# Second biases of a routed layer as one bf16 product a node tile, the second list ahead of the own rows, chosen rows scaled on ScalarE

## The chip, the cores and the metric

The kernel runs on one core of one Trainium2 chip. The core has a matrix engine (TensorE, PE in the profile; its weight loads are PEld), a vector engine (VectorE, DVE), an activation engine (ScalarE, ACT), GpSimd (POOL), which also issues the indirect DMAs (gathers and scatters by a list of rows), and SyncE (SP), which issues the plain DMAs. TensorE writes its results to PSUM, which has eight banks of 128 x 512 float32 here; VectorE and ScalarE read them from there. The metric is the device time of one execution in microseconds (us), as the median over runs.

## The reference

There are 1250 nodes with 512 features and 41250 edges. First comes a graph network of two layers, each of which takes for every node the maximum over its neighbours and multiplies it and the node itself by weights. Then comes a layer with 8 experts, and this is what the change touches:

```python
logits = x_flat @ Wr
probs = jax.nn.softmax(logits, axis=0)
vals, idx = jax.lax.top_k(probs.T, C)            # C = 512 nodes for each expert
selected = x_flat[idx]
h = gelu(einsum('ecd,edf->ecf', selected, W1) + b1[:, None, :])
out_e = einsum('ecf,efd->ecd', h, W2) + b2[:, None, :]
weighted = vals[..., None] * out_e
output = zeros_like(x_flat).at[idx.reshape(-1)].add(weighted.reshape(-1, Dd))
```

`x_flat` is the layer-normed result of the graph network. So each expert chooses the 512 nodes with its highest probabilities, works on these rows alone (512 to 256, Gelu, 256 to 512), and adds its rows, scaled with the probability, to the nodes that they came from. The result is added to the node's own `x`. The second bias `b2` of an expert enters a node as probability times `b2`, for every expert that chose the node.

## The kernel before

**Stages.** `fast_gnn` computes the graph network and ends at about 674 us. It leaves the rows `xs` (the tile `acc` in the profile), their layer norm in memory (`y_d`), and its transpose `yT`. `expert_choice` (line 1479) does the rest. The 1250 nodes are cut into ten tiles of 125 rows (`NT`, `TN`). A second form of the program for unusual graphs (`general_gnn`) stands behind a branch and doesn't run here.

**Routing, 674 to 721 us.** The threshold of each expert is found in eight rounds (line 1553). Each round counts on VectorE, sums with a small TensorE product (`pn`) and goes on with a few small VectorE operations. Then `chosen` (a 0 or 1 for each node and expert), each chosen node's place, and the lists are made. Between these steps `beside()` puts a piece of other TensorE work: the dense expert.

**The dense expert.** Expert 0 is computed for all nodes (`DENSE = 1`), by the generator `dense_steps` (line 1416). Each of its last ten pieces makes one tile of 125 rows: a product that puts the bias into a PSUM bank (`self.bias`), two products in float32 that add to it, and a ScalarE copy into `head.res` (the tile `xh`). A float32 product of 512 columns shows as two entries of TensorE.

**The bias product.** `fb` holds the eight second biases three times (partitions 0, 32 and 64), `bp` is their split into three bf16 parts whose sum is the float32 value, and `pick` is a matrix of zeros and ones. `pick[:, e]` times `bp` writes the bias of expert `e` into all rows of a bank (line 1518).

**Own rows.** `own_row(t)` (line 1690) adds `gate` (probability where chosen) times the dense expert's rows to `xs` on VectorE and stores the tile to `out` by two SP DMAs, one of 112 and one of 13 rows.

**The chosen experts, 1 to 7.** `listed(e)` (line 1662) makes the list of an expert: `pays` and `oh` on VectorE, ten small TensorE products into `pi`, then `got`, `idx` (the nodes) and `val` (their probabilities) on VectorE. The probabilities go through as three bf16 parts, which lie in `pay4` next to the node's number. `gathered` (line 1682) issues four gathers of 128 rows each on POOL. `expert` (line 1702) is a generator of two halves. The first half transposes the rows (`pt`, two banks, copied by ScalarE to `yselT`) and makes the hidden values (`ph`, then Gelu to `hT`). The second half makes four tiles of 128 rows: the bias product and two float32 products into `po`, a VectorE product by `val` into `oo`, and a scatter on POOL that adds the rows to `out`. Scatters of an expert wait for those of the expert before, and the first ones for the stores of the own rows.

**What sets the order.** Every engine is wrapped by `InOrder` (line 24), which keeps its instructions in the order in which they are written. The loop at line 1748 writes, for each expert: first half, (for expert 1 alone) the rest of the dense steps and the ten own rows, the next expert's list and gathers, second half. The banks `po` and `ph` and the small results of routing all come from the pool `ps_m`, tile name `pm`, with four banks in turn (line 1501); a product into a bank waits until the last reader of the bank's former content is done. `ps_t` has two banks for the transposes.

In the profile nearly all instructions have line 34, that of the `InOrder` wrapper, so groups are told apart by tile names. Memory that is reused shows under an older name: `ohs`, `xh`, `wroot` and `acc` hold the routing's and the dense expert's data.

Of the kernel before, what the change touches and what calls it, by code (L numbers as in the profile page):

```python
# [9 lines left out]
F32 = mybir.dt.float32  # L10
# [1282 lines left out]
class Routing:  # L1293
# [122 lines left out]
    def dense_steps(self):  # L1416


        dve, act, pe, pool, sp = self.engines
        TN, rows, KC, FC = self.sh["TN"], self.sh["rows"], self.KC, self.FC  # L1420
        NT = len(rows)
        cuts = [0, 4, 7, NT]
        for e in range(DENSE):
            w1, w2 = self.dense[e]
            for n, (t0, t1) in enumerate(zip(cuts, cuts[1:])):
                c0, w = t0 * TN, sum(rows[t0:t1])
                early = e == 0 and n < 2
                while early and any(t not in self.have for t in range(t0, t1)):
                    yield
                if early:  # L1430
                    both = self.wide[n]()
                for f in range(FC):
                    ph = both[f] if early else self.bank()
                    for k in range(KC):
                        pe.matmul(ph[:, :w], w1[:, k, f * P:(f + 1) * P], self.yT[:, k, c0:c0 + w],
                                  start=(k == 0), stop=(k == KC - 1))
                        if k == 1:
                            yield
                    if early:
                        self.waiting.append((e, f, c0, w, ph))  # L1440
                    else:
                        self.hidden(e, f, c0, w, ph)
                    yield
            for t in range(NT):
                r = rows[t]
                po = self.bank()
                self.bias(po[:r], e, r)
                for f in range(FC):
                    pe.matmul(po[:r], self.hT[:, f, t * TN:t * TN + r], w2[:, f, :],
                              start=False, stop=(f == FC - 1))  # L1450
                act.copy(self.res[e][:r, t, :], po[:r])
                yield

# [20 lines left out]
    def beside(self, n=1):  # L1474
        for _ in range(n):
            next(self.steps, None)


def expert_choice(tc, ctx, sh, xs, yT, y_d, out, head, flags=None):
# [22 lines left out]
    ps_x = ctx.enter_context(tc.tile_pool(name="ps_x", bufs=1, space=PSUM))  # L1502


    B3 = 96
    fb = rp.tile([P, D], F32, name="fb")
    pool.memset(fb[:B3], 0.0)
    for g in range(3):
        sp.dma_start(fb[32 * g:32 * g + E, :], sh["fb2"])
    bp = rp.tile([P, D], BF16, name="bp")  # L1510
    pick = rp.tile([P, E, P], BF16, name="pick")
    pool.memset(pick[:B3], 0.0)
    for g in range(3):
        pool.affine_select(out=pick[:B3], in_=pick[:B3], compare_op=ALU.not_equal, fill=1.0, base=-32 * g,
                           pattern=[[-1, E], [0, P]], channel_multiplier=1)

    def bias(po, e, r):
        pe.matmul(po, pick[:B3, e, :r], bp[:B3, :], start=True, stop=False)

    head.bias = bias  # L1520
    head.bank = lambda: ps_m.tile([P, D], F32, name="pm")

    weights = {}
# [158 lines left out]
    def gathered(idx):  # L1682
        ysel = rp2.tile([P, CC, D], F32, name="ysel")
        for c in range(CC):
            pool.indirect_dma_start(
                out=ysel[:, c, :], out_offset=None, in_=y_d[:, :],
                in_offset=bass.IndirectOffsetOnAxis(ap=idx[:, c:c + 1], axis=0))
        return ysel

    def own_row(t):  # L1690
        r = rows[t]
        for e in range(DENSE):
            dve.scalar_tensor_tensor(xs[:r, t, :], head.res[e][:r, t, :], gate[:r, t, e:e + 1], xs[:r, t, :],
                                     op0=ALU.mult, op1=ALU.add)
        cut = r - r % 16
        for p0, p1 in ((0, cut), (cut, r)):
            if p1 > p0:
                sp.dma_start(out[t * TN + p0:t * TN + p1, :], xs[p0:p1, t, :])
# [3 lines left out]
    def expert(e, idx, val, ysel):  # L1702
# [16 lines left out]
        yield  # L1719
        for c in range(CC):  # L1720
            po = ps_m.tile([P, D], F32, name="pm")
            bias(po, e, P)
            for f in range(FC):
                pe.matmul(po, hT[:, f, c * P:(c + 1) * P], w2[:, f, :],
                          start=False, stop=(f == FC - 1))
            oo = rp2.tile([P, D], F32, name="oo", bufs=4)
            dve.tensor_scalar_mul(oo, po, val[:, c:c + 1])
            add = pool.indirect_dma_start(
                out=out[:, :], out_offset=bass.IndirectOffsetOnAxis(ap=idx[:, c:c + 1], axis=0),
                in_=oo[:, :], in_offset=None, compute_op=ALU.add)  # L1730
# [13 lines left out]

    gate = rp.tile([P, NT, E], F32, name="gate")
    dve.tensor_mul(gate, chosen, pcol)
    beside(4)
    for e in range(DENSE, E):
        work = expert(e, *made, ysel)
        next(work)  # L1750
        if e == DENSE:

            for _ in head.steps:
                pass
            for t in range(NT):
                own_row(t)
        if e + 1 < E:

            made = listed(e + 1)
            ysel = gathered(made[0])  # L1760
        elif flags is not None:
            value = nc.values_load(flags[0:1, 0:1], min_val=0, max_val=1)
        next(work)
    return value

# [115 lines left out]
```

## Time and profile before

| what | value |
|---|---|
| median of 8 runs | 872.78 us (871.18 to 876.19) |
| the profiled execution's own time | 875.14 us |
| its span, first to last instruction | 873.4 us |
| mean granted clock of TensorE | 0.938 of full speed |
| busy: TensorE, VectorE, ScalarE, POOL | 697.3, 623.3, 208.6, 528.3 us |
| `oo` by VectorE, 28 of 128x512 | 21.0 us, 750 ns each |
| `hT` by ScalarE from PSUM, 14 of 128x512 | 9.6 us, 687 ns each |
| copies `xh<-pm` by ScalarE, 10 of 125x512 | 5.9 us, 586 ns each |
| scatters `out<-oo` on POOL, 28 | 44.8 us, 1601 ns each; the first expert's land in 5.4 to 6.0 us |
| last scatter issued | 858.02 us |

The profile is one execution of the program with all its instructions. Busy time counts an engine's running instructions; idle time in brackets, where a row has it, is the wait ahead of the instruction with what ended it. `out<-in` names the tile that is written and those that are read. The granted clock tells at which share of its full speed TensorE was let run.

### The profile page before, as it was taken

What the parts mean: (1) busy time and instruction counts of PE and PEld (TensorE: products, weight loads), DVE (VectorE), ACT (ScalarE), POOL (GpSimd) and SP (SyncE); (2) the same over time, 40 slices, a digit from 0 to 9 for tenths busy, and PEclk for the clock granted to TensorE, in tenths of its full rate; (3) what the DMA queues carried; (4) which work ended last, traced back from release to release, by engine and by line L of the source; (5) the groups of instructions that cost most, each with busy time, mean ns of one, the idle gap of its engine ahead of it and who ended that gap; (6) DMA issues with size and microseconds to landing.
All of it is one profiled execution on the core that took longest, in us unless ns stands there. A gap on an engine that the chain in (4) does not pass through costs nothing. (4 is left out here: it accounts for less than half of the span.)

```text
span 873.4 us, 8381 instructions
## 1 busy us (share of the span) xinstructions
PE 697.3 (80%) x2534; PEld 375.9 (43%) x2534; DVE 623.3 (71%) x1134; ACT 208.6 (24%) x349; POOL 528.3 (60%) x549
## 2 busy tenths in 40 slices
PE   0698867778888787998887889678668888999992
PEld 0344534444454433555444445334335544444440
DVE  6998799999999956469989899996543554332211
ACT  2644322334420132311100001002123322112110
POOL 7543777777777775077777777778701402566542
PEclk9999879999999798999999999989779899999997
DMA  7686557977877688258967878777731405777653
GB/s 173 201 263 205 131 176 173 229 227 239 260 221 225 190 257 264 70 182 179 226 212 221 275 242 282 239 224 256 241 114 48 146 0 170 185 174 186 125 98 51
DMA packets 67785, 165.47 MB, mean 189 GB/s; under 512 B 12918, under 2 KB 17588, under 8 KB 67730
## 3 DMA queue, kind: packets, MB, share of 16 engines
q0 software_dynamic: 37472, 114.19, 48.8%
q1 hardware_dynamic: 29438, 49.55, 17.5%
q10 hardware_dynamic: 820, 1.10, 0.5%
q8 instruction: 22, 0.36, 0.2%
q14 instruction: 33, 0.27, 0.1%
HBM read 136.35 MB, written 28.40 MB: 189 GB/s over the span
## 5 line engine op out<-in xcount | busy, mean ns | idle before, releaser
L34 POOL DMA_INDIRECT hb<-table_d,late_i x214 | 228.6, 1068 | 97.4 <-issue 56.3
L34 PEld LDWEIGHTS <-ohs 126*125 126x125 bf16 (+1 forms) x1221 | 169.0, 140 | 210.6 <-issue 134.0
L34 PE MATMUL pq<-xh,ohs 126*125 126x512 bf16 x816 | 202.7, 391 | 46.5 <-DVE acc L34 45.4
L34 POOL DMA_INDIRECT hb<-table_d,nat_i x140 | 147.4, 1053 | 60.2 <-issue 35.4
L34 DVE TENSOR_TENSOR acc<-acc,pq 125x1024 f32<-125x1024 f32 x122 | 148.6, 1218 | 25.1 <-PE pq L34 14.1
L34 PE MATMUL pair<-xh,ohs 126*125 126x512 bf16 x384 | 98.7, 395 | 28.2 <-DVE acc L34 28.2
L34 DVE TENSOR_TENSOR acc<-acc,pair 125x1024 f32<-125x1024 f32 x58 | 70.6, 1217 | 3.1 <-PE pair L34 0.4
L34 DVE TENSOR_TENSOR wide<-wide,hb 125x1024 f32<-125x1024 f32 (+1 forms) x60 | 71.4, 1189 | 1.8
L34 POOL DMA_INDIRECT ysel<-y_d,idx x28 | 27.7, 988 | 72.8 <-issue 29.7
L34 DVE TENSOR_TENSOR hb<-hb 125x1024 f32<-125x1024 f32 (+2 forms) x55 | 52.9, 962 | 22.1 <-DMA hb<-table_d,nat_i 14.6
L34 PE MATMUL pm<-wroot,turn 128*125 128x512 f32 x128 | 66.0, 600 | 0.4 <-ACT turn L34 0.4
L34 PE MATMUL pair<-wrel,turn 128*125 128x512 f32 x80 | 44.8, 712 | 13.0 <-ACT turn L34 9.8
L34 DVE TENSOR_TENSOR wide<-hb 125x1024 f32<-125x1024 f32 (+1 forms) x40 | 47.9, 1198 | 9.5 <-DMA hb<-table_d,nat_i 8.3
L34 POOL DMA_INDIRECT out<-oo,idx x28 | 44.8, 1601 | 15.8 <-DVE oo L34 8.1
L34 PE MATMUL pm<-yselT,w 128*128 128x512 f32 x112 | 49.9, 599 | 4.7 <-ACT yselT L34 4.7
L34 PE MATMUL pm<-w,hT 128*128 128x512 f32 x112 | 52.7, 591 | 0.0
L34 DVE TENSOR_SCALAR oo<-pm,val 128x512 f32<-128x512 f32 x28 | 21.0, 750 | 44.0 <-PE pm L34 44.0
L34 PE MATMUL pm<-wrel,turn 128*125 128x512 f32 x80 | 44.3, 706 | 4.5 <-DVE acc L34 4.5
L34 ACT COPY line<-pm 125x512 f32<-125x512 f32 x16 | 9.4, 585 | 114.9 <-PE pm L34 114.9
L34 DVE COPY got<-pi 128x20 f32<-128x20 f32 x7 | 1.2, 178 | 49.7 <-PE pi L34 49.7
L34 PEld LDWEIGHTS pm<-yselT,w 128*128 128x128 f32 x112 | 20.7, 190 | 29.8 <-issue 23.4
L34 PE MATMUL pair<-ident,acc 125*128 125x125 f32 x48 | 8.7, 312 | 31.1 <-DVE acc L34 15.5
(272 smaller groups left out, 919.5 us busy)
## 6 DMA issues: line engine op xcount, KB each, us to landing
w<-in_fw SPq DMA_DIRECT2D x14, 512.0 KB
ohs<-idx_d SPq DMA_DIRECT2D x10, 615.2 KB
root_d<-line SPq DMA_DIRECT2D x20, 250.0 KB
ahead<-root_d SPq DMA_DIRECT2D x20, 250.0 KB
table_d<-acc SPq DMA_DIRECT2D x20, 224.0 KB
ovf_d<-line SPq DMA_DIRECT2D x18, 224.0 KB
hb<-table_d,late_i POOLq DMA_INDIRECT x214, 4.8
ohs<-in_x SPq DMA_DIRECT2D x10, 250.0 KB
```

What stands on the lines that cost most here:

```text
L34: made = call(*args, **kwargs)
```

## The change

Three things change in `expert_choice` and `dense_steps`.

The bias products leave the dense steps and the chosen experts; there the first float32 product now starts the bank (`start=(f == 0)`), and `pick` goes. In their place each node tile gets one product: `shares` holds for every node the probabilities of the experts that chose it, as three bf16 parts, repeated three times in blocks of 32 columns. `shares` is transposed by ten products with a bf16 unit matrix `eye` into `sharesT`, by way of `ps_t` and ScalarE copies. `own_row(t)` multiplies `sharesT` of its tile with `bp`, which now holds each part of the biases three times, and adds the result (a bank of `ps_m`) to the rows. So a node gets the biases of all its experts at once, with its own row.

In the loop the list and the gathers of the next expert are written ahead of the rest of the dense steps and the own rows; for expert 1 this puts expert 2's list in front of them.

The chosen rows are scaled by ScalarE (`activation` with `Identity` and `scale`) in place of VectorE.

```diff
@@ dense_steps
                 po = self.bank()
-                self.bias(po[:r], e, r)
                 for f in range(FC):
                     pe.matmul(po[:r], self.hT[:, f, t * TN:t * TN + r], w2[:, f, :],
-                              start=False, stop=(f == FC - 1))
+                              start=(f == 0), stop=(f == FC - 1))
@@ expert_choice
+    assert 3 * E <= 32
     B3 = 96
     fb = rp.tile([P, D], F32, name="fb")
     pool.memset(fb[:B3], 0.0)
     for g in range(3):
-        sp.dma_start(fb[32 * g:32 * g + E, :], sh["fb2"])
+        for k in range(3):
+            sp.dma_start(fb[32 * g + E * k:32 * g + E * k + E, :], sh["fb2"])
     bp = rp.tile([P, D], BF16, name="bp")
-    pick = rp.tile([P, E, P], BF16, name="pick")
-    pool.memset(pick[:B3], 0.0)
-    for g in range(3):
-        pool.affine_select(out=pick[:B3], in_=pick[:B3], compare_op=ALU.not_equal, fill=1.0, base=-32 * g,
-                           pattern=[[-1, E], [0, P]], channel_multiplier=1)
-
-    def bias(po, e, r):
-        pe.matmul(po, pick[:B3, e, :r], bp[:B3, :], start=True, stop=False)
-
-    head.bias = bias
+    eye = rp.tile([P, P], BF16, name="eye")
+    pool.memset(eye, 0.0)
+    pool.affine_select(out=eye, in_=eye, compare_op=ALU.not_equal, fill=1.0, base=0,
+                       pattern=[[-1, P]], channel_multiplier=1)
+    shares = rp.tile([P, NT, 3, 32], BF16, name="shares")
+    pool.memset(shares, 0.0)
@@ own_row
         r = rows[t]
+        po = ps_m.tile([P, D], F32, name="pm")
+        pe.matmul(po[:r], sharesT[:B3, t, :r], bp[:B3, :], start=True, stop=True)
         for e in range(DENSE):
             dve.scalar_tensor_tensor(xs[:r, t, :], head.res[e][:r, t, :], gate[:r, t, e:e + 1], xs[:r, t, :],
                                      op0=ALU.mult, op1=ALU.add)
+        dve.tensor_add(xs[:r, t, :], xs[:r, t, :], po[:r])
@@ expert
             po = ps_m.tile([P, D], F32, name="pm")
-            bias(po, e, P)
             for f in range(FC):
                 pe.matmul(po, hT[:, f, c * P:(c + 1) * P], w2[:, f, :],
-                          start=False, stop=(f == FC - 1))
+                          start=(f == 0), stop=(f == FC - 1))
             oo = rp2.tile([P, D], F32, name="oo", bufs=4)
-            dve.tensor_scalar_mul(oo, po, val[:, c:c + 1])
+            act.activation(oo, po, AF.Identity, scale=val[:, c:c + 1])
@@ expert_choice, the end
     gate = rp.tile([P, NT, E], F32, name="gate")
     dve.tensor_mul(gate, chosen, pcol)
+    for i in range(3):
+        dve.tensor_tensor(shares[:, :, :, E * i:E * i + E],
+                          chosen.unsqueeze(2).to_broadcast([P, NT, 3, E]),
+                          pay4[:, :, :, 2 + i].unsqueeze(2).to_broadcast([P, NT, 3, E]), op=ALU.mult)
     beside(4)
+    sharesT = rp.tile([P, NT, P], BF16, name="sharesT")
+    for t0 in range(0, NT, KC):
+        n = min(KC, NT - t0)
+        pt = ps_t.tile([P, KC, P], F32, name="pt")
+        for k in range(n):
+            pe.matmul(pt[:B3, k, :], shares[:, t0 + k].rearrange("p j i -> p (j i)"), eye, start=True, stop=True)
+        act.copy(sharesT[:B3, t0:t0 + n, :], pt[:B3, :n, :])
     for e in range(DENSE, E):
         work = expert(e, *made, ysel)
         next(work)
+        if e + 1 < E:
+
+            made = listed(e + 1)
+            ysel = gathered(made[0])
+        elif flags is not None:
+            value = nc.values_load(flags[0:1, 0:1], min_val=0, max_val=1)
         if e == DENSE:
 
             for _ in head.steps:
                 pass
             for t in range(NT):
                 own_row(t)
-        if e + 1 < E:
-
-            made = listed(e + 1)
-            ysel = gathered(made[0])
-        elif flags is not None:
-            value = nc.values_load(flags[0:1, 0:1], min_val=0, max_val=1)
         next(work)
```

## The prediction

> **What bounds the kernel now.** I read the clock and the 40 slices first. In the last quarter TensorE is near full while VectorE falls to 1 to 3 tenths.
>
> ```profile
> PE   0698867778888787998887889678668888999992
> DVE  6998799999999956469989899996543554332211
> PEclk9999879999999798999999999989779899999997
> ```
>
> Next I read the timeline of a chosen expert in steady state. Columns: start, us, engine, operation.
>
> ```profile
> 764.51 0.38 PE L34 MATMUL pm<-bp,pick 96*128 96x512 bf16 x1
> ...
> 764.73 1.88 PE L34 MATMUL pm<-w,hT 128*128 128x512 f32 x4
> ...
> 766.45 1.04 PE L34 MATMUL pt<-ident,ysel 128*128 128x128 f32 x8
> 766.65 0.75 DVE L34 TENSOR_SCALAR oo<-pm,val 128x512 f32<-128x512 f32 x1 [1.18 <-PE pm L34]
> ...
> 767.14 1.07 ACT L34 COPY yselT<-pt 128x512 f32<-128x512 f32 x2 [7.80 <-PE pt L34]
> ...
> 767.78 1.14 PE L34 MATMUL pt<-ident,ysel 128*128 128x128 f32 x8 [0.29 <-ACT yselT L34]
> ...
> 769.60 7.13 PE L34 MATMUL pm<-yselT,w 128*128 128x512 f32 x16 [0.68 <-ACT yselT L34]
> ...
> 784.57 1.04 PE L34 MATMUL pt<-ident,ysel 128*128 128x128 f32 x8
> ```
>
> From 766.45 to 784.57 is one period, 18.12 us, and TensorE idles in it only about 1 us, for ScalarE's copies of the transposes (0.29 + 0.68). A bias product costs 764.73 - 764.51 = 0.22 us; four a period. The `oo` scaling on VectorE hangs beside this path.
>
> Then the place where the own rows and the second list lie:
>
> ```profile
> 721.27 0.23 DVE L34 TENSOR_TENSOR gate<-chosen,pcol 128x80 f32<-128x80 bf16 x1
> 721.62 4.73 DVE L34 SCALAR_TENSOR_TENSOR acc<-xh,gate,acc 125x512 f32<-125x512 f32 x7
> ...
> 728.79 0.75 DVE L34 SCALAR_TENSOR_TENSOR acc<-xh,gate,acc 125x512 f32<-125x512 f32 x1 [1.13 <-ACT xh L34]
> 729.46 0.36 DVE L34 TENSOR_TENSOR pays<-ohs,col 128x200 bf16<-128x200 bf16 x1
> 729.74 1.48 DVE L34 TENSOR_TENSOR oh<-ohs,lane 128x1280 bf16<-128x1280 bf16 x1
> ...
> 733.41 7.13 PE L34 MATMUL pm<-yselT,w 128*128 128x512 f32 x16 [0.67 <-ACT yselT L34]
> ...
> 740.39 0.40 PE L34 MATMUL pi<-pays,oh 128*128 128x20 bf16 x10
> ...
> 740.82 0.18 DVE L34 COPY got<-pi 128x20 f32<-128x20 f32 x1 [9.60 <-PE pi L34]
> 740.86 1.88 PE L34 MATMUL pm<-w,hT 128*128 128x512 f32 x4
> ```
>
> VectorE does all ten own rows while TensorE still works on the dense expert, then `pays` and `oh`, and then stands 9.60 us until TensorE reaches the list's product (`pi`), which is written behind expert 1's first half. So `got`, the list's next step, can't run before 740.8.
>
> Last, the granted clock by windows (columns: window, length, then busy time of each engine, clock):
>
> ```profile
> 688.00:693.00 5.00, 3.29 (x13) 1.89 (x13) 4.04 (x13) 0.68 (x6) 0.00 (x0) 1.00 0.02 7
> 693.00:696.40 3.40, 2.98 (x9) 2.11 (x10) 2.45 (x11) 0.83 (x5) 0.19 (x1) 0.51 0.00 0
> 696.40:699.80 3.40, 3.40 (x7) 1.96 (x8) 2.27 (x8) 0.41 (x1) 1.88 (x6) 0.50 0.00 0
> ...
> 716.80:720.20 3.40, 1.43 (x4) 0.35 (x2) 3.21 (x6) 0.59 (x1) 0.00 (x0) 1.00 0.01 2
> 720.30:723.70 3.40, 3.40 (x15) 1.75 (x16) 2.82 (x9) 0.00 (x0) 1.57 (x2) 0.51 0.13 36
> 723.80:727.20 3.40, 3.40 (x10) 1.53 (x9) 3.40 (x6) 1.18 (x2) 2.75 (x3) 1.00 0.87 275
> ```
>
> A stretch in which TensorE was busy for 1.43 of 3.40 us was followed by 3.4 us at half clock, one of 3.29 of 5.00 us by 6.8 us at half clock.
>
> **The change, part by part.** Times are those of the profiled execution, 875.14 us own time for a span of 873.4, 0.3% over the median of eight runs, 872.78; differences are carried over to the median.
>
> *Set-up.* Out go the memset of `pick` (0.95) and three selects (3.42) on POOL; in come an `eye` of 128 columns (an eighth of such a select and memset, about 0.3) and a memset of `shares`, 960 wide (0.9 by the 1024 of `pick`). SP issues 9 small loads instead of 3, 1.24/3 = 0.41 each, so 2.5 us more, and POOL's split of the bias (679.12 to 684.67) waits for them: it ends near 687 in place of 684.9. Behind it is only `pcol`'s memset, needed at 691.3; the expert weights behind the loads are needed at 733. Cost 0; if `pcol` were late, the excess over 4 us.
>
> *Dense bias products.* Ten of 0.22 leave TensorE. They count where a small product of the routing chain waited behind them: at 704.18 (its operand was ready at 703.17), 711.44, 713.54 and 715.82, so 4 x 0.22 = -0.9 us at the first list. The next three lie partly at half clock: -0.9 more on TensorE before expert 1's transposes.
>
> *`shares` and `sharesT`.* Three VectorE products of 240 bf16 elements, 0.4 each (0.36 for the 200 of `pays`, 0.48 for 320), after `idx`, in time VectorE now has free. Ten small TensorE products (under 0.1 each) and three ScalarE copies (0.59, 0.59, about 0.38) stand ahead of expert 1's transposes and use their two banks. Today the transposes wait for the gathered rows up to 732.11, the last landing 5.8 us after its issue beside the row stores; without these stores I take the median 3.9, so 725.3 + 3.9 = 729.2. Then the banks decide: dense work ends 726.5, three copies to 728.7, four transposes with copies behind them at about 0.9 to 731.9. The first half starts at 731.95 in place of 733.41: -1.5, and -0.9 if the landing stays late.
>
> *The list ahead of the own rows, and the rows' new product.* This is the dear part. The list moves `pays`, `oh`, ten TensorE products, `got`, `idx`, two `val` and four gathers ahead of ten rows. The gathers pass nothing on POOL and start 1.5 us earlier. On VectorE the rows now stand behind `got`, so behind TensorE's 740.39 - 1.5 = 738.9; `val` ends at 741.48 - 1.5 = 740.0. Each row is a multiply-add (0.68 to the next, 4.73/7) and a new add from PSUM (0.69 for 125x512 adds, 0.72 to a dependent one): 1.40, ten rows 14.0 us. Each row's bias product takes a `pm` bank, of which there are four, and the bank comes free only with the row's add. TensorE therefore advances one product per 1.40 us, and the first `po` of expert 1's second half needs the bank of row 7, free at 740.05 + 7 x 1.40 = 749.85. What is queued behind: the second half, and all later experts. It starts at 749.95 and takes 4 x 1.71 (1.93 less 0.22) = 6.8, ending 756.8, where expert 2's transposes began at 748.38. So +8.4 us at full clock, between +7.8 (rows at 1.36, by two independent pitches) and +9.7 (rows at 1.50, as `oo` takes 0.75 each, and only -0.9 before). The row stores on SP (20 x 0.41) end near 755 and land a few us later, so expert 1's scatters start near 758 in place of 746.5, take 4 x 1.9 and land 5.5 later, near 771; expert 2's scatters come at 776. SP's next weight load slips from 740.6 to about 755 for expert 4, which runs near 798. Both cost 0.
>
> *The clock after the stall.* For some 9 us TensorE does 0.22 in each 1.40, emptier than the stretch that halved the clock. When the second half starts the clock is half, and stays so 3.4 to 6.8 us by the two cases above; half of that is lost: +1.7 to +3.4, I take the middle, +2.6. It could be 0 if the clock held.
>
> The Trainium skill (TensorE: Matmul & The Clock Gate, part 1) has the clock halve after at least one idle window of about 3.4 us and return after one busy window. Read strictly, a stall with a product every 1.4 us is no idle window, and the sum without the clock term would be +4.5; the rows above show it halving with TensorE busy 1.43 of 3.40 us, so I go by the rows.
>
> *Experts 2 to 7.* 24 bias products less: 24 x 0.215 = -5.2. Of this the last expert's first is lost and some 0.1 elsewhere, since the second hidden half (849.25 + 0.69) is then what TensorE waits for: +0.3. `oo` on ScalarE: with `scale` from PSUM it lies between the copy's 0.59 and the identity's 0.81, nearest the Gelu's 0.69. The fourth one of an expert stands ahead of the next expert's first copy (766.65 + 0.62, its spacing, against 767.14): +0.15 on each of six transitions, 0.07 to 0.25 by the ends: +0.9. No table load stands before the identities after Sqrt or Exp; whether one is needed after Gelu no row shows. If so, two of 1.28 an expert fall into ScalarE's idle 3.85 and 7.8: 0 to +0.3. Sum -3.9 (-4.4 to -3.2).
>
> Together 8.4 + 2.6 - 3.9 = +7.1: own time 882.2, median 879.9.
>
> **The rivals.** *No stall* (ends faster): the rows' adds keep out of TensorE's way, by VectorE doing them in its idle time before 740. Then -1.5 - 0.9 - 3.9 = -6.3: 866.5. It decides if the rows are worked before `got`, or three banks more were there. For it: operands are ready by 729. Against: every engine follows the written order above. 10%.
> *Stall, but the clock holds or returns at once*: +4.5, 877.3. Against: 0.51 at 720 to 723.7. 18%.
> *Dearer*: rows at 1.50, a late first half, 6.8 us of half clock, poor gain after: 9.7 + 3.4 - 3.2 = +9.9, 882.7, more if weights or scatters slip past their margins of 5 us and more. 8%.
> *Bank wait partly covered*, so that stall and gain cancel (a stall near 5 us): within 0.2%, 4%.
>
> **How the numbers follow.** The forecast case (878 to 882) has 60%. The sound range is 874 to 884: below it lie "no stall" and half of the cancelling case, above it a part of the dearer one. 0.2% (1.75 us) is about what a measurement tells from no change: faster 0.11, same 0.04, slower 0.85.
>
> **What would show it.** Right: `got` of the second list ahead of the own rows, near 739; `pm<-bp` products spaced 1.4 us with TensorE idle for VectorE's add; half clock from about 750; a period of 17.4 in place of 18.12; no wait of the second scatters. Wrong: rows between 722 and 737, a table load in each expert, or a period that is not shorter because ScalarE's copies come later.

## The result and the profile after

The changed kernel takes 896.92 us (median of 16 runs, 891.36 to 902.35); the kernel before, run beside it, takes 872.37 (46 runs). The ratio is 1.0273 (95% interval 1.0257 to 1.029): 24 us slower. The direction was forecast, the size was not: the forecast was 879.9, with 884.0 as the upper end.

The profiled execution has a span of 895.6 us in place of 873.4, at a granted clock of 0.929 in place of 0.938. The 40 slices of the page of after (PE and DVE in tenths busy, the granted clock in tenths):

```profile
PE   0697976778898779997886896796688887878991
DVE  7898799999999856599997999976435625111100
PEclk9999889999999989999998999897888997988996
```

In the last nine slices TensorE has 7s and 8s where it had 8s and 9s, and the clock falls to 8 and 7 where it was 9. So the time was lost among the chosen experts. Four marks in both timelines cut the loss up:

| stretch | before | after | difference |
|---|---|---|---|
| first list's product to second list's product | 20.15 | 19.12 | -1.0 |
| second list's product to expert 2's transposes | 7.99 | 20.58 | +12.6 |
| expert 2's transposes to the last scatter's issue | 109.64 | 123.34 | +13.7 |
| first list's product to the last scatter's issue | 137.8 | 163.0 | +25.2 |

In this execution the graph stage also ended 3.7 us earlier (670.54 against 674.27), which has nothing to do with the change, and the routing took 0.7 us less; after the last scatter 16.8 us follow instead of 15.4. -3.7 - 0.7 + 25.2 + 1.4 = +22.2, the difference of the spans.

**The second stretch is the forecast stall.** The timeline of after around the own rows (start, us, engine, operation, and in brackets the idle time before it and what ended it):

```profile
734.92 0.40 PE L34 MATMUL pi<-pays,oh 128*128 128x20 bf16 x10
735.36 0.18 DVE L34 COPY got<-pi 128x20 f32<-128x20 f32 x1 [15.53 <-PE pi L34]
...
736.84 0.69 DVE L34 TENSOR_TENSOR acc<-acc,pm 125x512 f32<-125x512 f32 x1
737.44 0.75 DVE L34 SCALAR_TENSOR_TENSOR acc<-xh,gate,acc 125x512 f32<-125x512 f32 x1
...
737.58 0.38 PE L34 MATMUL pm<-bp,sharesT 96*125 96x512 bf16 x1 [1.34 <-DVE acc L34]
...
744.85 0.59 PE L34 MATMUL pm<-bp,sharesT 96*125 96x512 bf16 x1 [0.87 <-DVE acc L34]
...
746.31 9.36 PE L34 MATMUL pm<-w,hT 128*128 128x512 f32 x16 [0.87 <-DVE acc L34]
...
755.50 1.04 PE L34 MATMUL pt<-ident,ysel 128*128 128x128 f32 x8
```

The rows begin behind `got`, and TensorE gets one product per row: from 737.58 to 744.85 are five rows, 1.455 us each, and each product waits for VectorE's add (`<-DVE acc`). The second half starts 11.39 us behind the list's product and takes 9.36 us where the same sixteen entries elsewhere take 7.11. The windows over the stall (window, length, busy time of PE, PEld, DVE, ACT, POOL, then the granted clock, DMA share, GB/s) say why:

```profile
740.00:742.00 2.00, 0.59 (x2) 0.19 (x2) 1.90 (x4) 0.00 (x0) 0.72 (x1) 0.64 0.95 322
742.00:744.00 2.00, 1.11 (x2) 0.31 (x2) 1.90 (x3) 0.00 (x0) 0.00 (x0) 0.50 0.93 305
...
750.00:752.00 2.00, 2.00 (x5) 0.83 (x4) 2.00 (x3) 0.69 (x1) 0.00 (x0) 0.80 0.65 192
752.00:755.50 3.50, 3.50 (x9) 1.47 (x8) 0.29 (x1) 1.38 (x2) 0.00 (x0) 1.00 0.60 187
```

The clock halves while TensorE does one small product per row (0.50 at 742) and comes back at about 751.

**The third stretch is what was not forecast.** It was to shrink by 3.9 us and grew by 13.7. One period in the timeline of after, from an expert's second half to the next one's first:

```profile
786.87 0.40 PE L34 MATMUL pi<-pays,oh 128*128 128x20 bf16 x10
...
787.12 7.11 PE L34 MATMUL pm<-w,hT 128*128 128x512 f32 x16
...
788.15 1.48 DVE L34 TENSOR_TENSOR oh<-ohs,lane 128x1280 bf16<-128x1280 bf16 x1
788.47 2.06 POOL L34 DMA_INDIRECT ysel<-y_d,idx  x1 [7.77 <-PE pm L34]
...
793.37 0.94 POOL L34 DMA_INDIRECT ysel<-y_d,idx  x1 [0.30 <-issue]
...
794.07 1.04 PE L34 MATMUL pt<-ident,ysel 128*128 128x128 f32 x8
...
795.78 0.63 PE L34 MATMUL pt<-ident,ysel 128*128 128x128 f32 x4 [0.67 <-DMA ysel<-y_d,idx]
...
799.72 1.09 PE L34 MATMUL pt<-ident,ysel 128*128 128x128 f32 x4 [3.31 <-DMA ysel<-y_d,idx]
```

TensorE now waits for gathered rows: 0.67 us for the third chunk, 3.31 for the fourth. The fourth gather was issued at 793.37 and its rows were used at 799.72, 6.35 us later. In the period of before that the prediction shows no such wait stands. Its other rows are these (timeline of before; a list's product, the first and the fourth gather, the next list's `oh`):

```profile
758.45 0.40 PE L34 MATMUL pi<-pays,oh 128*128 128x20 bf16 x10
...
760.05 1.02 POOL L34 DMA_INDIRECT ysel<-y_d,idx  x1 [5.75 <-PE pm L34]
...
763.91 0.94 POOL L34 DMA_INDIRECT ysel<-y_d,idx  x1 [0.31 <-issue]
...
767.59 1.48 DVE L34 TENSOR_TENSOR oh<-ohs,lane 128x1280 bf16<-128x1280 bf16 x1
```

The fourth gather is issued at 763.91, and its transposes, the last four of the eight in the row at 767.78, start at 768.27, 4.36 later. In after there are six waits for gathers, 10.1 us together. Behind the longest three (1.94, 3.31 and 2.93 us) the clock halves as well: the first halves that follow take 8.72, 9.08 and 9.39 us in place of 7.13. The windows of the periods show it (same columns):

```profile
755.50:772.90 17.40, 16.34 (x59) 8.01 (x58) 2.26 (x6) 6.16 (x10) 11.04 (x8) 1.00 0.77 154
772.90:794.10 21.20, 18.09 (x60) 8.69 (x59) 2.26 (x6) 6.26 (x10) 11.30 (x9) 0.92 0.67 149
794.10:817.60 23.50, 18.85 (x60) 9.06 (x58) 2.26 (x6) 6.26 (x10) 11.05 (x9) 0.85 0.58 132
```

The first period has the forecast length, 17.4 us. The next take 21.2 and 23.5, the latter at a mean clock of 0.85.

Three things in the rows above come together. `oh`, the next list's big product, now starts right behind `val` at 788.15; before, it stood behind the fourth `oo` (767.59, after 766.65). POOL's first gather runs beside it and takes 2.06 us; before, it took 1.02 (760.05). So the fourth gather starts 1.0 us later in the period. And the second half has lost four bias products, 0.86 us, so its rows are wanted that much earlier. Then SP issues a weight load of 512 KB, which waits for the end of the second half (timeline of SP of after):

```profile
794.27 0.37 SPq L34 DMA_DIRECT2D w<-in_fw  x1
```

That is 0.9 us behind the fourth gather; before, the same load was 2.7 us behind it (766.64 against 763.91).

### The profile page after: what moved, and what is told of

It reads as the page before. It is cut to its first block, busy times and chain, and to the rows that moved or that the text cites. A ratio compares the mean times of both kernels' runs of the same rounds, so it can differ in the third digit from the quotient of the medians.

```text
span 895.6 us, 8375 instructions
## 1 busy us (share of the span) xinstructions
PE 699.1 (78%) x2516; PEld 376.2 (42%) x2516; DVE 612.3 (68%) x1119; ACT 228.9 (26%) x380; POOL 529.0 (59%) x548
## 5 line engine op out<-in xcount | busy, mean ns | idle before, releaser
L34 POOL DMA_INDIRECT ysel<-y_d,idx x28 | 32.3, 1153 | 78.1 <-PE pm L34 36.3
L34 POOL DMA_INDIRECT out<-oo,idx x28 | 44.3, 1581 | 30.9 <-ACT yselT L34 17.4
L34 PE MATMUL pm<-yselT,w 128*128 128x512 f32 x112 | 55.7, 655 | 4.7 <-ACT yselT L34 4.7
L34 PE MATMUL pair<-wrel,turn 128*125 128x512 f32 x80 | 42.2, 676 | 12.7 <-ACT turn L34 9.4
L34 PE MATMUL pm<-wrel,turn 128*125 128x512 f32 x80 | 42.2, 676 | 4.0 <-DVE acc L34 4.0
L34 PEld LDWEIGHTS pm<-yselT,w 128*128 128x128 f32 x112 | 23.0, 211 | 33.6 <-issue 26.9
L34 PE MATMUL pair<-ident,acc 125*128 125x125 f32 x48 | 9.1, 323 | 32.8 <-DVE acc L34 17.3
L34 PEld LDWEIGHTS pm<-w,hT 128*128 128x128 f32 x112 | 21.5, 197 | 28.3 <-issue 22.4
```

Source lines behind the costliest of these rows:

```text
L34: made = call(*args, **kwargs)
```

## The experiments

The theories that the expectations name: **A**, `oo` leaving VectorE lets `oh` run beside the first gather, which makes the gathers late, and then they share the time with the weight load; **B**, the shorter second half alone uses up the gathers' slack; **C**, late row stores push weight loads and scatters into the gathers. Ratios are to the kernel before, run on the same chip. The column "stage" goes from the first list's product to the last scatter's issue in the profiled execution (before: 137.8 us, after: 163.0); "period" is the distance between the products of two lists in the later experts (before: 18.12, after: 21.2, 23.5, 23.6, 18.7).

| kernel | median, us | ratio (95%) | stage | period |
|---|---|---|---|---|
| changed, `oo` back on VectorE | 880.27 | 1.0091 (1.0064 to 1.0118) | 145.9 | 17.4 |
| before, `oo` on ScalarE alone | 875.93 | 1.0035 (1.001 to 1.006) | 142.0 | 18.6 |
| before, list ahead of the rows alone | 882.15 | 1.0101 (1.0066 to 1.0136) | 150.5 | 18.12 |
| before, rows' product alone | 883.03 | 1.0114 (1.0075 to 1.0153) | 149.6 | 17.4 |
| changed, one `oo` of four on VectorE | 949.97 | 1.0091 (1.004 to 1.0143) | 146.4 | 17.5 |
| changed, no late weight loads | 959.68 | 1.0257 (1.0182 to 1.0332) | 150.6 | 18.5 |
| first one, rows spread over both halves | 949.35 | 1.0151 (1.0096 to 1.0205) | 141.3 | 17.5 |
| first one, rows in the first half | 939.32 | 1.0059 (1.0011 to 1.0107) | 136.65 | 17.5 |
| the last, list in the middle of that half | 868.28 | 0.9948 (0.9927 to 0.9969) | 134.65 | 17.5 |
| the last, `oo` on ScalarE | 867.93 | 0.9936 (0.9908 to 0.9964) | 135.9 | 17.65 |
| changed, list in the middle of the half | 880.51 | 1.0089 (1.0055 to 1.0123) | 146.2 | 17.65 |

Rows five to eight ran on a chip on which the graph stage of every kernel took some 75 us longer (before: 945 to 947 us) and varied more; there the stage says more than the median. The stage itself is read from one profiled execution of each kernel.

### The changed kernel with `oo` back on VectorE

```diff
-            act.activation(oo, po, AF.Identity, scale=val[:, c:c + 1])
+            dve.tensor_scalar_mul(oo, po, val[:, c:c + 1])
```

> The changed kernel with one line put back: oo is scaled by VectorE again. Theory A (the 17 us beyond the forecast come from oo leaving VectorE: the next list's oh then runs beside the first gather of the present list, that gather takes 2.06 us in place of 1.02, all four land later and beside a weight load, TensorE waits and its clock halves): the first gather of every expert takes 1.02 us again, periods after the second expert are 17.2 to 17.7 us instead of 21.2 to 23.5, time 876 to 881 us; the stall of 12.6 us in front of expert 1's second half stays. Theory B (the shorter second half alone uses up the slack of the gathers, 0.85 us): TensorE waits for gathers in each period, periods above 19 us, time 888 us or more. Theory C (the late row stores push weight loads and scatters into the gathers of all later experts): time unchanged at 893 to 900 us.

Measured: 880.27 us, 17 below the changed kernel and close to the 879.9 that was forecast for the changed kernel. The timeline of one period of this kernel:

```profile
784.11 7.11 PE L34 MATMUL pm<-w,hT 128*128 128x512 f32 x16
...
785.46 1.01 POOL L34 DMA_INDIRECT ysel<-y_d,idx  x1 [4.14 <-PE pm L34]
...
789.32 0.95 POOL L34 DMA_INDIRECT ysel<-y_d,idx  x1 [0.30 <-issue]
...
791.05 1.04 PE L34 MATMUL pt<-ident,ysel 128*128 128x128 f32 x8
...
792.20 1.48 DVE L34 TENSOR_TENSOR oh<-ohs,lane 128x1280 bf16<-128x1280 bf16 x1
792.39 1.25 PE L34 MATMUL pt<-ident,ysel 128*128 128x128 f32 x8 [0.29 <-ACT yselT L34]
```

The first gather is short again, `oh` stands behind the fourth `oo` at 792.20, and the transposes wait for ScalarE's copy alone. The fourth gather is at 5.21 us into the second half (789.32 - 784.11); in the changed kernel it was at 6.25 (793.37 - 787.12). In the whole stage TensorE waits 0.21 us for gathers. The second half is just as short as in the changed kernel, so B alone is refuted, and one line carries 17 us. The stall stays (second half 9.42 us, half clock).

### Only `oo` on ScalarE, in the kernel before

```diff
-            dve.tensor_scalar_mul(oo, po, val[:, c:c + 1])
+            act.activation(oo, po, AF.Identity, scale=val[:, c:c + 1])
```

> The kernel before with one line changed: oo is scaled by ScalarE; biases and order as before. Theory A: oh runs beside the first gather, which takes about 2.06 us; the fourth gather lands about 1.04 us later than before, past a slack of 0.85 us, and nearer to the weight load that starts when the second half ends; waits of 0.2 to 3 us an expert, time 875 to 890 us. Theory B: the second half has its old length, so the gathers keep their slack: 871 to 874 us. Theory C: 871 to 874 us.

Measured: 875.93 us, 1.0035. The timeline of one period, with a row of the next:

```profile
758.14 1.48 DVE L34 TENSOR_TENSOR oh<-ohs,lane 128x1280 bf16<-128x1280 bf16 x1
...
758.46 2.06 POOL L34 DMA_INDIRECT ysel<-y_d,idx  x1 [6.13 <-PE pm L34]
...
767.18 0.63 PE L34 MATMUL pt<-ident,ysel 128*128 128x128 f32 x4 [0.20 <-DMA ysel<-y_d,idx]
...
785.21 1.15 PE L34 MATMUL pt<-ident,ysel 128*128 128x128 f32 x8 [0.72 <-ACT yselT L34]
```

The long first gather is there at once, and costs little: three waits of 0.20 to 0.35 us. Periods are near 18.6 in place of 18.12, but one without any wait for a gather is as long (18.56); there TensorE waits 0.72 us for ScalarE's copy of the transposes (785.21) where before it waited 0.29, so most of what a period gains is ScalarE's. Of the stage's 4.2 us, 1.9 lie ahead of the second list's product (22.03 against 20.15), in a first half that ran partly at half clock before any `oo`. With the bias products still in the second half the gathers have the time. So the loss of 17 us takes both, the later gather and the shorter second half.

### One `oo` of four on VectorE

If it is `oh`'s place and not ScalarE's work, the third of the four is enough to hold `pays` and `oh` back:

```diff
-            act.activation(oo, po, AF.Identity, scale=val[:, c:c + 1])
+            if c == 2:
+                dve.tensor_scalar_mul(oo, po, val[:, c:c + 1])
+            else:
+                act.activation(oo, po, AF.Identity, scale=val[:, c:c + 1])
```

> The changed kernel with only the third of an expert's four oo on VectorE, the other three on ScalarE. The next list's pays and oh stand behind that one and start some 6 us after val, when the gathers are out. Theory A (oh beside the first gather is the cause, not who scales the rows): first gather 1.02 us, periods 17.3 to 17.8 us, 877 to 882 us as with all four on VectorE. If ScalarE's share of the scaling were itself the cost (its copies of the transposes come later), three quarters of the loss stays: 890 us or more.

Measured: first gather 1.01 us, no wait for gathers, periods of 17.5, stage 146.4. Three of the four on ScalarE cost nothing that the stage shows (146.4 against 145.9); what the one on VectorE does is hold back `oh`.

### No weight loads behind expert 3's

This kernel leaves out the weights of experts 4 to 7, which work with those of experts 1 to 3.

```diff
-        w1, w2 = weights.pop(e)
+        w1, w2 = weights[DENSE + (e - DENSE) % 3]
...
-        fetch(e + 2)
+        if e + 2 <= DENSE + 2:
+            fetch(e + 2)
```

> The changed kernel, but experts 4 to 7 load no weights and work with those of experts 1 to 3 (part of the computation is left out: the output belongs to other weights). Theory A with its second part (the fourth gather is so late because the weight load at the end of the second half runs beside it): the first gather still takes 2.06 us, but the fourth lands about 3.6 us after its start instead of more than 6, TensorE waits about 1 us an expert, the clock mostly stays up: periods 18.0 to 19 us, 882 to 888 us. If the loads don't matter: periods of 21 to 23.5 us as before, 893 to 900 us.

Measured: stage 150.6 and periods of 18.5. The time doesn't show the gain: its ratio, 1.0257 (1.0182 to 1.0332), is about that of the changed kernel (1.0273, on other chips), where 1.01 to 1.02 was expected (882 to 888 us); it comes from four runs on the chip on which times vary more. So this experiment rests on the timeline and the stage. A period without a load:

```profile
860.65 2.06 POOL L34 DMA_INDIRECT ysel<-y_d,idx  x1 [4.99 <-PE pm L34]
...
865.55 0.94 POOL L34 DMA_INDIRECT ysel<-y_d,idx  x1 [0.30 <-issue]
...
869.31 0.63 PE L34 MATMUL pt<-ident,ysel 128*128 128x128 f32 x4 [0.81 <-DMA ysel<-y_d,idx]
870.61 7.13 PE L34 MATMUL pm<-yselT,w 128*128 128x512 f32 x16 [0.67 <-ACT yselT L34]
```

The gather is as long and late as in the changed kernel, but its rows are used 3.76 us after the issue (869.31 - 865.55) instead of 6.35; TensorE waits 0.81 and the first half keeps its 7.13 us. Of the 17.1 us between the changed kernel (163.0) and the one with `oo` on VectorE (145.9), 12.4 go with the loads (163.0 - 150.6) and 4.7 stay, with the later gather and ScalarE's `oo`. The changed kernel has a witness of its own: its last loads are issued at 817.79, and the next gathers have none beside them. They start with the long one (timeline of POOL, after), and the transposes that follow wait 0.61 us; the list after that is the last, has no `oh` beside it, and its first gather is short:

```profile
835.76 2.06 POOL L34 DMA_INDIRECT ysel<-y_d,idx  x1 [10.17 <-PE pm L34]
...
854.41 1.02 POOL L34 DMA_INDIRECT ysel<-y_d,idx  x1 [5.24 <-PE pm L34]
```

### The list ahead of the rows, alone

The block that makes the next list and gathers moves ahead of the own rows in the kernel before; the rows have no bias product.

```diff
         next(work)
+        if e + 1 < E:
+            made = listed(e + 1)
+            ysel = gathered(made[0])
         if e == DENSE:
             ...
             for t in range(NT):
                 own_row(t)
-        if e + 1 < E:
-            ...
```

> The kernel before with the second list and its gathers written ahead of the own rows, nothing else. The rows have no bias product, so no bank of TensorE waits for them: they run 741.5 to 748.3 us on VectorE and expert 1's oo behind them. Theories A and B: 871 to 876 us, since oo waits at most 4 to 5 us on four banks and the list of expert 3 still stands behind oo. Theory C: row stores and weight loads are late here as well (stores end near 750 instead of 733), so gathers wait in all later experts and the time is 880 us or more.

Measured: 882.15 us, outside the 871 to 876 of A and B and in the range of C, though gathers are late by microseconds for expert 3 alone and not in all later experts. The timeline:

```profile
743.62 5.07 SPq L34 DMA_DIRECT2D out<-acc  x9
...
755.39 1.65 POOL L34 DMA_INDIRECT out<-oo,idx  x1 [13.41 <-DMA w<-in_fw]
...
756.70 0.40 PE L34 MATMUL pi<-pays,oh 128*128 128x20 bf16 x10
...
762.98 1.02 POOL L34 DMA_INDIRECT ysel<-y_d,idx  x1 [0.30 <-PE pm L34]
...
767.14 0.63 PE L34 MATMUL pt<-ident,ysel 128*128 128x128 f32 x4 [2.29 <-DMA ysel<-y_d,idx]
```

The rows, now behind `got`, end late, and so do their stores on SP (still being issued at 743.62 and after). Expert 1's first scatter, which has to wait for them, stands on POOL until 755.39 (the row names a weight load that ended at the same time), and the next gathers stand behind it in POOL's order: the first is issued 6.28 us behind its list's product (762.98 - 756.70), where before it is 1.60 (760.05 - 758.45). TensorE waits 2.29, 1.99 and 0.44 us and then runs a first half of 9.79 us at half clock. That period takes 26.83 us, the later ones 18.12 as before. That is theory C for one expert; the forecast had put late stores at nothing. In the changed kernel C doesn't act: there the first expert's scatters are issued from 757.18 to 764.5, before the list's product at 765.71, because the stall has delayed that as well.

### The rows' product, alone

Bias products out, rows' product in, list behind the rows as before, `oo` on VectorE: the changed kernel with the line of the first experiment and the list's block moved back.

```diff
-        if e + 1 < E:
-            ...
         if e == DENSE:
             ...
             for t in range(NT):
                 own_row(t)
+        if e + 1 < E:
+            made = listed(e + 1)
+            ysel = gathered(made[0])
         next(work)
```

> The biases as in the changed kernel (one product a node tile), but the second list behind the own rows as before and oo on VectorE. The ten products of the rows stand ahead of the second list on TensorE and VectorE, so the list starts only when the rows are done: the second half of expert 1 starts about 15 us late and the second gathers about 14 us late, in part beside it. All theories: slower than the run with oo put back, 882 to 890 us; if the move of the list were itself the cost of the stall, this run would be the faster one.

Measured: 883.03 us. The stall is there without the move, and the list's product waits for it too: it stands at 751.47 behind a wait of 6.91 us for `oh`, and the second half follows at 751.76, where it is at 746.96 with the list ahead. No gather is waited for. So the stall comes from the rows' product, and the move of the list makes it 3.7 us cheaper (145.9 against 149.6), where alone it costs 12.7 (150.5 against 137.8).

### Rows spread over both halves of expert 1

From the kernel with `oo` on VectorE: the next `pays` and `oh` come first, and the ten rows are written one by one between the pieces of expert 1, so that TensorE has work while VectorE adds. The edit also moves the rest of the dense steps ahead of the loop, and it holds expert 1's four scatters back until the last of its four `oo` is written; the lines below don't show these two.

```diff
+    def slot(e, n=1):
+        if e == DENSE:
+            for t in left_rows[:n]:
+                own_row(t)
+            del left_rows[:n]
@@ expert
+        slot(e, 2)
         for c in range(CC):
             ...
+            if c % 2:
+                slot(e)
...
+                if k == 1 or (k == KC - 1 and f == 0):
+                    slot(e)
...
             po = ps_m.tile([P, D], F32, name="pm")
+            slot(e)
```

> Biases as in the changed kernel, oo on VectorE, and the ten own rows with their products written between the pieces of expert 1's two halves (two ahead of the transposes, two within, three between the hidden products, three between the tiles of the second half), the pays and oh of the second list right after shares, got after seven rows. If the stall comes from ten rows standing on four banks behind got, it goes: the second half of expert 1 starts within 1 us of the second list's product, the clock stays full, and the periods stay at 17.4 us. Then 880.3 less 12.6 and a shorter last piece of the first half, plus 10 x 0.22 of products on TensorE: 866 to 870 us, faster than both kernels. If rows cost the same wherever they are put: 878 us or more.

Measured: the stall is gone (second half at 803.52 behind the list's product at 803.02), and stage 141.3 in place of 145.9. The time misses what was expected (faster than both kernels): its ratio is 1.0151. For the rows end in the second half, their stores are late, expert 1's first scatter waits 8.16 us until 817.16, and the next gathers stand behind the scatters:

```profile
824.74 1.02 POOL L34 DMA_INDIRECT ysel<-y_d,idx  x1 [0.30 <-issue]
...
829.00 0.37 SPq L34 DMA_DIRECT2D w<-in_fw  x1
...
830.32 2.01 PE L34 MATMUL pt<-ident,ysel 128*128 128x128 f32 x12 [1.35 <-DMA ysel<-y_d,idx]
```

The list's product was at 821.61, the first gather comes 3.1 us later, a weight load lies beside the last one, TensorE waits 1.35 and 2.10 us, and one period takes 24.1: C again. How much of this comes from holding the scatters back was not run by itself.

### All rows in the first half

The rows' multiply-adds (`dense_row`) are split from their product, add and stores (`own_row`); seven of them stand ahead of the loop, three inside, and the ten products lie between the pieces of the first half (three ahead of the transposes, three between them, four between the hidden products). The scatters are no longer held back; `pays`, `oh` and the dense steps stand ahead of the loop as in the run above.

```diff
+    def dense_row(t):
+        ...
     def own_row(t):
-        for e in range(DENSE):
-            dve.scalar_tensor_tensor(xs[:r, t, :], ...)
         ...
+    for t in range(7):
+        dense_row(t)
@@ expert
+        slot(e, 3)
...
+            if c:
+                slot(e)
...
+                if k == 1 or k == (2 if f else KC - 1):
+                    slot(e)
```

> As the run with rows between the pieces, but all ten rows within the first half of expert 1: the dense multiply-adds ahead of it, where VectorE is free, the products three ahead of the transposes, three between them, four between the hidden products, each with its add and stores. The row stores then start some 8 us earlier, so expert 1's scatters and behind them expert 3's gathers on POOL are not late. If the stall came from banks behind got, and the 24.1 us period of the run before from late row stores ahead of the scatters, both go: from the first list's product to the last scatter about 134 us instead of 137.8 (kernel before), 145.9 (oo put back alone) and 141.3 (rows between), all periods 17.3 to 17.6 us, time 0.3 to 0.7% under the kernel before. If a period above 18 us stays, the gathers have no slack for another reason, and the time is that of the kernel before or more.

Measured: stage 136.65, below that of before (137.8) but not the 134 expected: at expert 2 stand a wait of 0.98 us for gathers and a first half of 8.83, and that period takes 19.89, the others 17.3 to 17.6. The expectation had named a period above 18 as the sign that gathers are still short of slack, with no gain in time, and so it came. The time itself says nothing clear: medians of 939.32 against 945.15, a ratio over the rounds of 1.0059, and runs of the kernel before from 928.9 to 953.3.

### The list in the middle of the first half's second product

```diff
@@ expert
                 for k in range(KC):
                     ...
+                    if f == FC - 1 and k == 1:
+                        yield
...
-        yield
```

So the loop writes the next list and its gathers some 1.7 us earlier.

> As the run with the rows early, and for every expert the next list's product and gathers written after the second of the four products of the second hidden half, 1.7 us earlier on TensorE. The gathers get 1.7 us of slack at no cost. Theory A: no wait for a gather anywhere, periods 17.2 to 17.5 us, from the first list's product to the last scatter 132 to 134.5 us (kernel before 137.8), 0.4 to 0.8% under the kernel before. If gathers are late for another reason than their start, waits for them stay.

Measured: 868.28 us, 0.9948 (0.9927 to 0.9969): half a per cent under the kernel before, as expected. Periods are 17.5 but for expert 3's of 19.07, where gathers are still waited for (0.54 and 0.70), so the stage of 134.65 lies a little above the 132 to 134.5 expected.

### The same with `oo` on ScalarE

```diff
-            dve.tensor_scalar_mul(oo, po, val[:, c:c + 1])
+            act.activation(oo, po, AF.Identity, scale=val[:, c:c + 1])
```

> The run with the list in the middle of the half, with oo on ScalarE again for all experts, which cost the changed kernel 17 us. Theory A: oh runs beside the first gather again, which takes 2.06 us, but the 1.04 us are within the new slack of 1.7 us: waits for gathers under 0.3 us an expert, periods 17.3 to 17.8 us, within 0.3% of the run with oo on VectorE. If ScalarE's scaling costs by itself, or the slack isn't the point: periods of 18.5 us and more, 8 us or more above that run.

Measured: 867.93 us. The first gather takes 2.06 us again, and in the later experts nothing waits for it; only at expert 2 gathers are waited for (0.67 and 0.29, more than the 0.3 expected). Periods are 17.65, 0.15 above those with `oo` on VectorE, and the stage is 1.3 longer. So the one line that cost 17 us in the changed kernel costs nothing here that the time shows (the two intervals overlap).

### The changed kernel with the earlier list alone

Only the `yield` of the changed kernel moves, as two runs above; stall and ScalarE's `oo` stay.

> The changed kernel itself, with the place where the loop takes over moved from the end of the second hidden half to its middle, so that the next list's product and gathers (and expert 1's own rows) come 1.7 us earlier; oo stays on ScalarE, oh stays beside the first gather, the rows stay on four banks. Theory A: the first gather still takes 2.06 us, but no expert waits for gathers more than 0.3 us, periods 17.4 to 17.8 us, and only the stall in front of expert 1's second half is left, 1 to 2 us shorter: 876 to 881 us. If the 17 us beyond the forecast have another cause than the gathers' slack, 888 us or more.

Measured: 880.51 us, 1.0089. From the first list's product to expert 2's transposes it takes 39.15 us, in the changed kernel 39.70, so the stall is hardly shorter (1 to 2 us were expected); the gain lies behind it. The timeline of a period:

```profile
767.39 1.49 DVE L34 TENSOR_TENSOR oh<-ohs,lane 128x1280 bf16<-128x1280 bf16 x1
767.71 2.06 POOL L34 DMA_INDIRECT ysel<-y_d,idx  x1 [2.34 <-issue]
...
772.60 0.94 POOL L34 DMA_INDIRECT ysel<-y_d,idx  x1 [0.30 <-issue]
...
775.21 1.04 PE L34 MATMUL pt<-ident,ysel 128*128 128x128 f32 x8
...
776.68 1.14 PE L34 MATMUL pt<-ident,ysel 128*128 128x128 f32 x8 [0.43 <-ACT yselT L34]
```

`oh` and the long first gather are as before this edit, but the fourth gather now starts 2.61 us ahead of the transposes (772.60, 775.21) instead of 0.70 (793.37, 794.07), and all they wait for is ScalarE (0.43). Two edits of different kinds, this one and the first, both give the gathers their time back, one by an earlier start and one by a shorter first gather, and both take back 17 us.

## Why the prediction was wrong

**Right: the stall.** The forecast had the second half 11.05 us behind the second list's product (738.9 to 749.95) and expert 2's transposes 20.5 behind it; measured 11.39 and 20.58. Rows cost 1.455 us where 1.40 was taken. The half clock cost 9.36 - 7.11 = 2.25 us where 2.6 was taken. The forecast's reading of the clock held too: the row at 742 says 0.50. The Trainium skill (TensorE: Matmul & The Clock Gate, part 1) has the clock halve after at least one idle window of about 3.4 us; here it halved with a small product every 1.455 us.

**Right: the small parts.** Set-up cost nothing: `pcol`'s memset ran at 682.30 and its result was needed at 687.60. The routing took 0.7 us less (0.9 forecast), the first half came 1.7 earlier (1.5 forecast). `oo` on ScalarE takes 0.69 us, with no table load in the expert's timeline, and adds 0.2 to a period (17.65 against 17.4; 0.15 forecast), though 0.43 in the kernel before (0.72 against 0.29), above the 0.25 that the forecast allowed.

**Wrong: the step "Experts 2 to 7", -3.9 us; measured +13.7.** Its terms, -5.2, +0.3 and +0.9, make -4.0, a tenth from the sum as written. The bias products go the right way and fall short by 1.4: with `oo` on VectorE this stretch takes 106.2 us, 3.5 less than before, where -4.9 was due. The failed term is the move of `oo`: put at +0.9, it cost 17.1 (stage 163.0 against 145.9). The step said that the scaling "on VectorE hangs beside this path" and priced only what ScalarE does with it. But on VectorE it also held something: `pays` and `oh` of the next list are written behind it, and ran only when the gathers were issued. In after `oh` starts 1.28 us behind the product of the list before it (788.15 - 786.87), in the kernel before 9.14 (767.59 - 758.45): beside the first gather instead of behind the last. The step that would have caught it is to ask what stands behind the removed instruction on its engine, and what that meets.

**The bound that was missing.** The forecast took the gathers' margin for granted. The trace of before held it: fourth gather at 763.91, rows wanted at 768.27, and 3.76 us needed where no load follows closely (the run without late loads), so by estimate 0.6 us of slack. The shorter second half alone takes 0.86, which leaves 0.3 short, and the run with `oo` on VectorE shows one wait of 0.21. The longer first gather takes 1.0 more. What is then short, about 1.3 us (0.86 + 1.0 - 0.6), grows by the weight load, whose issue stays bound to the end of the second half and so moves next to the gather, and by the clock behind waits of 2 to 3 us.

**The rivals.** The forecast case itself is what two of the runs measure (880.27 and 880.51, forecast 879.9): kernels with the same stall in which the gathers keep their slack. The clock didn't hold, and nothing covered the bank wait, so those two rivals are out. "Dearer" had the right sign of the miss but named weights and scatters, not gathers, with 5 us of margin. "No stall" was put at 866.5 if the rows are worked before `got`; the version that does this, with the gathers' slack restored, takes 867.93 (beside 873.76 for the kernel before on that chip). And the list of what would prove the forecast wrong had a period that isn't shorter "because ScalarE's copies come later": the period was longer, but the rows name the gathers.

What stays open: the 1.4 us more behind the last scatter, and why the fourth gather needs 4.80, 6.35 and 5.89 us in the three periods with a load close behind it; only that it falls to 3.76 without one is shown.

## What to carry to other kernels

When an instruction leaves an engine, list what is written behind it on that engine: it will start earlier, and may run beside something that it used to follow. For a transfer that is hidden, work out its slack from the trace of before (issue, landing, first use) and hold every microsecond that the change takes off the cover against it; a saving on the path is a loss of cover. A gather that starts one microsecond later can cost four to six (periods of 21.2 to 23.6 against 17.4) when another transfer is tied to the same event and the clock drops while TensorE waits.

## What the runs showed of the hardware

In the later experts the first gather of four occupied POOL for 2.06 us when it was issued 0.3 us into VectorE's `oh` (bf16, two inputs from SBUF, 1.48 us), and for 1.01 or 1.02 otherwise; a scatter issued 0.3 us into it took 2.64 instead of about 1.6 (792.50 in the kernel with `oo` back on VectorE). The stretch goes with what is left of `oh`: in the kernel before, a scatter with 0.68 us of it left took 2.12 (750.33), and one with 0.10 left 1.56 (768.97). The Trainium skill (SBUF — State Buffer, Who interferes with whom) says that a VectorE instruction with two SBUF inputs contends with a GpSimd instruction that reads SBUF. The rows of `oh` agree, if issuing a gather or a scatter counts as such a read. The own rows' multiply-adds, with two float32 inputs from SBUF, don't settle it: a gather issued 0.08 us into one took 0.95 (736.01, after), one issued 0.21 us into one took 1.41 (721.83, before).

The fourth gather needed 3.76 us from issue to use with no load beside it, and 4.80, 6.35 and 5.89 with a 512 KB load issued 0.7 to 0.9 us behind it. And TensorE's wait of 3.31 us was followed by a first half of 9.08 us in place of 7.13.
